# Up projection of groups two to four in seven block products, with the gate's sums of x and cached weight sums

## The chip, the cores and the metric

The kernel runs on one core of a Trainium2 chip. The metric is the device time of one execution in microseconds, the median of three runs. Inputs and outputs are float32; matmuls take float32r operands.

## The reference

The part that matters here is the first block's gated projection with a sparsity step: per row of s, the half of the entries that are smallest in magnitude is set to zero.

```python
s = silu(einsum('bsh,ih->bsi', x, w_gate))          # x: 2 x 1024 x 1024, w: 2752 x 1024
_, idx = top_k(-abs(s), k)                          # k = 1376 of 2752
s = s with the entries idx of each row set to 0
s = s * einsum('bsh,ih->bsi', x, w_up)
x = layernorm(x + einsum('bsi,hi->bsh', s, w_down))
# then a second block: low-rank-adapted feed-forward on x, and another layernorm
```

## The kernel before

**Tiling.** The 2048 rows are 16 tiles of 128, in four groups of four tiles. A group is worked on as two pairs of tiles. The 2752 columns are eight blocks of 344 (`BW`), taken as four block pairs `u` = 0 to 3. The contraction over 1024 is halved. So for a tile pair and a block pair, x and the weight are each 2x2 blocks: `A11` to `A22` of x, `B11` to `B22` of the weight.

**Products.** `products` multiplies one block of x (for both tile pairs) with one weight block. Every float32 operand is split into a rounded high part and a remainder (`split`: a cast on ScalarE, line 173, and a subtraction, line 174, mostly on GpSimd), and three of the four combinations are multiplied: 24 matmuls of 128x344 for one x block and one weight block over two tile pairs (line 353). Gate (other than group one's first block pair) uses seven block products for the eight of a plain 2x2 product: it multiplies blocks and sums of blocks of x (`S1` to `S4`) with blocks and sums of the weight (`T1` to `T4`), and `post` adds the products up from PSUM. Up uses the plain form: four steps of two block products each, 48 matmuls a step, and `up` multiplies the PSUM result with the gate's result.

**Steps.** `gate_up` (line 283) goes through a list of steps (group, block pair, gate or up, step). At each step it starts weight loads up to five steps ahead (`w_load`, into three raw slots `wr`), prepares weights up to three steps ahead (`w_prep`: cast and subtraction, into four slots each of `wh` and `wl`), emits the matmuls, and empties PSUM. PSUM has four pair buffers. A framework orders the instructions of each engine from this program order; what is emitted earlier has precedence where both are ready.

**Weight sums.** In group one, `w_prep` forms T1 to T4 of the gate's weights on VectorE and writes them to device memory: as one float32 tensor for the first block pair, as high and low parts for the other three. Later groups load them: the first block pair's are split again, the others go straight into `wh` and `wl` (line 258).

**Sums of x.** `x_raw` loads the next group's x into buffers that top-k has left, and `x_slot` forms one operand (sums on VectorE, cast on ScalarE, subtraction on VectorE). For the next group this happens in the last block pair, at the steps that the table `XAT` names.

**Top-k.** `topk` (line 417) is a generator. While group g is projected, it works on group g-1, one piece at each call: it loads the group's s, takes absolute values, makes six passes that count per row how many entries lie below a threshold (three tiles by a sign activation with accumulation on ScalarE, line 460, one on VectorE, line 463) and update the threshold, then selects by two VectorE operations per tile (lines 497 and 500), writes the mask (line 513), and checks the counts by a register read (lines 518 to 534). Its pieces are held behind the latest split and the latest PSUM reads by `behind`. `gate_up` calls it from the first step of a group's first block pair:

```python
for _ in range(2 if w == "u" and k % 2 == 0 else 1):
    if self.tkg:
        next(self.tkg, None)
```

All loads and stores are on SP's queue, in order. After `gate_up` come the down projection, its layernorm and the second block, which the change does not touch but for the steps at which the first three masks of the down projection are prepared.

Of the kernel before, what the change touches and what calls it, by code (L numbers as in the profile page):

```python
# [7 lines left out]
F = mybir.dt.float32  # L8
# [5 lines left out]
ALU = mybir.AluOpType  # L14
# [4 lines left out]
P = 128  # L19
# [18 lines left out]
T0 = 0.7528  # L38
SLOPE = 0.000528
TKAT = (0, "g", 0)  # L40
CACHED = ("T1", "T2", "T3", "T4")
# [5 lines left out]
WDG = 0  # L47
XAT = {"raw": (("g", 4), ("g", 5), ("g", 6), ("u", 0)), ("u", 0): ("S2",), ("u", 1): ("S1", "S3", "S4"), ("u", 2): ("A11", "A21"), ("u", 3): ("A12", "A22")}
WARM = 48
# [16 lines left out]
class Kern:  # L66
# [8 lines left out]
    def run(self):  # L75
# [3 lines left out]
        with ExitStack() as es:  # L79
# [14 lines left out]
            for i in range(8):  # L94
# [12 lines left out]
                (u, b): [self.dram.tile([P, CW], F, name=f"tw{u}{b}{n}") for n in "hl"] for u in range(NU) for b in CACHED  # L107
            }
            self.q1, self.q2, self.x2 = [], [], {}
            ps_es = ExitStack()  # L110
# [71 lines left out]
    def x_raw(self, g):  # L182
# [7 lines left out]
        for h in range(1 if g else 2):  # L190
# [8 lines left out]
            if g == 0 and h == 0:  # L199
                yield  # L200

    def x_slot(self, op):
        V, sub = self.nc.vector, ALU.subtract
# [14 lines left out]
    def form(self, i):  # L218
        g, u, w, k = self.steps[i]
        return 0 if w == "u" or g + u == 0 else 2 if g == 0 else 1  # L220

    def w_load(self, i):
# [12 lines left out]
        if f == 2:  # L235
            if k == 0:
                self.wb = {q: load(q) for q in G0}
            self.wraw.append(self.wb)
        elif f and u == 0 and b in CACHED:
            r = self.wr.get()  # L240
            self.lastd = nc.sync.dma_start(r, self.tw_d[u, b][0])
            self.wraw.append(r)
        elif f and b in CACHED:
            self.wraw.append(None)
        else:
            self.wraw.append(load(b))

    def w_prep(self, i):
# [21 lines left out]
        if g + u == 0 and w == "g" and k:  # L270
# [3 lines left out]
            for o, x, y in ((), T_AT[0], T_AT[1] + T_AT[2], T_AT[6])[k]:  # L274
                V.tensor_tensor(self.tt[o], self.b0[x], self.b0.get(y, self.tt.get(y)), ALU.subtract)
        if (g, u, w, k) == (0, 0, "u", 3):
            for o in CACHED:
                nc.sync.dma_start(self.tw_d[0, o][0], self.tt[o])
        if f == 2 and b in CACHED:
            for x, d in zip(hl, self.tw_d[u, b]):  # L280
                nc.sync.dma_start(d, x.bitcast(F))

    def gate_up(self):
        nc, V = self.nc, self.nc.vector
        ng = self.nt // GT
        self.steps = [(g, u, w, k) for g in range(ng) for u in range(NU) for w in "gu" for k in range(7 if w == "g" and g + u else 4)]
        self.xfull, self.tkg, self.xs, self.xraw, self.wraw, self.wq, self.li, self.wi = {}, None, {}, {}, [], [], 0, 0
# [4 lines left out]
        for i, (g, u, w, k) in enumerate(self.steps):  # L292
# [35 lines left out]
            if u == NU - 1 and g + 1 < ng:  # L328
                if (w, k) == XAT["raw"][0]:
                    self.xg = self.x_raw(g + 1)  # L330
                for _ in range(XAT["raw"].count((w, k))):
                    next(self.xg, None)
                for op in XAT.get((w, k), ()):
                    with self.behind():
                        self.x_slot(op)
# [21 lines left out]
    def post(self, un, k, x, cc):  # L357
# [734 lines left out]
```

## Time and profile before

| what | value |
|---|---|
| median of three runs | 1923.47 us (1922.35 to 1924.25) |
| profiled execution | 1926.91 us, span 1925.1 us |
| mean granted TensorE clock | 0.993 |
| TensorE busy | 1885.3 us, 10825 matmuls |
| line 353 (gate and up), three forms | 1928 matmuls each, 14.0 to 929.4 us from the span's start |
| VectorE, ScalarE, GpSimd busy | 1229.6, 904.0, 973.0 us |
| traffic | 488.66 MB, 254 GB/s over the span |

Times in the profile are microseconds from the start of one profiled execution. A group's row gives how often it ran, the busy time and the mean of one in ns, and after the bar the idle time of its engine just ahead of it with what ended it. A matmul's mean includes the time in which it overlaps its neighbours. A window's row gives the busy time of each engine in that stretch, the number of instructions in brackets, the granted clock, the share of the DMA engines' time and GB/s. A timeline's row gives start, duration, engine, line, operation, and in brackets the idle time ahead and what ended it.

### The profile page before, as it was taken

The page shows a single profiled execution, that of the slowest core. Times are in us where ns is not written, and L with a number is a line of the kernel's source. Part 1 is how long each engine was busy: PE and PEld are TensorE (multiplying, and loading weights), DVE is VectorE, ACT ScalarE, POOL GpSimd, SP SyncE. Part 2 cuts the span into 40 slices and gives each one's busy share as a digit, 9 for nine tenths or more (in the row PEclk, how much of TensorE's full clock was granted, in tenths as well). Part 3 has the DMA queues.
Part 4 walks back from the last instruction along what each step waited for, and adds up shares of the span by engine and source line. Part 5 has one row for each costly group of instructions (what it writes and reads, how often), then busy time and mean ns, then how long its engine had stood idle before and what let it go on. Part 6 is the DMA issues. An engine that isn't in the chain of part 4 may idle for free. (4 is left out here: it accounts for less than half of the span.)

```text
span 1925.1 us, 29381 instructions
## 1 busy us (share of the span) xinstructions
PE 1885.3 (98%) x10825; PEld 1754.4 (91%) x10825; DVE 1229.6 (64%) x1831; ACT 904.0 (47%) x1448; POOL 973.0 (51%) x606
## 2 busy tenths in 40 slices
PE   9999999999999999999999999999998999998998
PEld 9999999999999999999888787888787979898896
DVE  4633556767358574691238998688467857779565
ACT  4333477414883258622246533323333746557362
POOL 5655664445445354355565443554565746436062
PEclk9999999999999999999999999999999999999999
DMA  7677687676977868667798756977776878485651
GB/s 266 237 250 260 236 325 261 210 272 253 330 231 241 314 235 303 236 228 256 282 328 285 270 188 227 337 245 261 268 250 244 279 284 321 155 318 177 229 196 66
DMA packets 166205, 488.66 MB, mean 254 GB/s; under 512 B 24772, under 2 KB 45380, under 8 KB 166056
## 3 DMA queue, kind: packets, MB, share of 16 engines
q1 hardware_dynamic: 165848, 486.43, 71.9%
q8 instruction: 85, 1.39, 0.3%
q14 instruction: 64, 0.52, 0.1%
q10 hardware_dynamic: 208, 0.31, 0.0%
HBM read 370.30 MB, written 116.33 MB: 253 GB/s over the span
## 5 line engine op out<-in xcount | busy, mean ns | idle before, releaser
L174 POOL TENSOR_TENSOR wl<-wr,wh 128x1376 fp32r<-128x1376 f32 (+2 forms) x187 | 566.4, 3035 | 466.1 <-ACT wh L173 436.8
L353 PE MATMUL mm<-wh,xh 128*128 128x344 f32 x1928 | 610.4, 322 | 2.8 <-DMA wh<-tw3T1h 2.8
L353 PE MATMUL mm<-wh,xl 128*128 128x344 f32 x1928 | 609.8, 320 | 0.0
L173 ACT CAST wh<-wr 128x1376 fp32r<-128x1376 f32 (+2 forms) x192 | 232.4, 1215 | 340.9 <-PE mm L353 199.6
L353 PEld LDWEIGHTS mm<-wh,xh 128*128 128x128 f32 x1928 | 364.7, 189 | 3.0 <-issue 3.0
L353 PEld LDWEIGHTS mm<-wh,xl 128*128 128x128 f32 x1928 | 364.6, 189 | 0.0
L353 PE MATMUL mm<-wl,xh 128*128 128x344 f32 x1928 | 342.1, 319 | 0.0
L353 PEld LDWEIGHTS mm<-wl,xh 128*128 128x128 f32 x1928 | 310.1, 188 | 0.0
L765 PE MATMUL mm<-wh,mh 128*128 128x512 f32 x680 | 217.8, 400 | 0.1
L765 PE MATMUL mm<-wl,mh 128*128 128x512 f32 x680 | 215.1, 395 | 1.1 <-POOL wl L174 1.1
L765 PE MATMUL mm<-wh,ml 128*128 128x512 f32 x648 | 205.5, 396 | 0.8 <-DVE ml L750 0.8
L460 ACT ACTIVATE jk<-a,cur 128x2752 int8<-128x2752 f32 x66 | 170.8, 2588 | 31.2 <-DVE cur L482 15.8
L994 POOL TENSOR_TENSOR hf<-hf,gt 128x344 f32<-128x344 f32 x96 | 142.2, 1491 | 75.6 <-DVE gt L988 68.7
L725 POOL TENSOR_TENSOR m<-m,ub 128x512 f32<-128x512 f32 (+2 forms) x93 | 111.0, 1194 | 128.0 <-ACT ub L724 65.8
L981 PE MATMUL mm<-wh,fh 128*128 128x344 f32 x512 | 166.2, 325 | 5.8 <-DVE gt L988 5.2
L983 PE MATMUL mm<-wh,fl 128*128 128x344 f32 x512 | 164.0, 320 | 0.0
L982 PE MATMUL mm<-wl,fh 128*128 128x344 f32 x512 | 163.9, 320 | 0.0
L765 PEld LDWEIGHTS mm<-wl,mh 128*128 128x128 f32 x680 | 127.4, 188 | 30.1 <-POOL wl L174 2.2
L768 DVE TENSOR_TENSOR acc<-acc,mm 128x1024 f32<-128x1024 f32 x96 | 116.4, 1214 | 57.9 <-PE mm L765 27.8
L765 PEld LDWEIGHTS mm<-wh,mh 128*128 128x128 f32 x680 | 124.7, 189 | 24.8 <-ACT mh L749 0.5
L765 PEld LDWEIGHTS mm<-wh,ml 128*128 128x128 f32 x648 | 121.2, 189 | 26.9 <-DVE ml L750 1.0
L992 ACT ACTIVATE pa<-pa 128x344 f32<-128x344 f32 x256 | 123.0, 483 | 38.6 <-DVE pa L990 34.0
(191 smaller groups left out, 2742.5 us busy)
## 6 DMA issues: line engine op xcount, KB each, us to landing
wr<-wu SPq DMA_DIRECT2D x64, 688.0 KB
wr<-wg SPq DMA_DIRECT2D x52, 688.0 KB
wr<-wd SPq DMA_DIRECT2D x48, 512.0 KB
s_d<-cc SPq DMA_DIRECT2D x64, 344.0 KB
m_d<-mt SPq DMA_DIRECT2D x64, 344.0 KB
a<-s_d SPq DMA_DIRECT2D x64, 344.0 KB
wl<-wc_w SPq DMA_DIRECT2D x48, 344.0 KB
wh<-wc_w SPq DMA_DIRECT2D x48, 344.0 KB
```

The lines of the kernel that those rows point to most:

```text
L173: self.lasta = self.nc.scalar.copy(hi, raw)
L174: (eng or self.nc.gpsimd).tensor_tensor(lo, raw, hi.bitcast(F), ALU.subtract)
L353: self.nc.tensor.matmul(o, l, r, start=start and n < m and n % (2 * KH) == 0, stop=stop and n >= m and (n - m) % KH == KH - 1)
L460: nc.scalar.activation(jk.bitcast(I8), av[j], AF.Sign, bias=t, scale=-1.0, accum_out=s)
L725: nc.gpsimd.tensor_tensor(m[:, :w], m[:, :w], ub[:, :w], ALU.mult)
L765: nc.tensor.matmul(ps[:, h], a, b[:, h * 512 : (h + 1) * 512], start=i == 0, stop=i == len(ops) - 1)
L768: nc.vector.tensor_tensor(out, out, ps.rearrange("p a b -> p (a b)"), ALU.add)
L981: nc.tensor.matmul(o, fh[:, c, :], wh[:, c, :], start=c == 0, stop=False)
L982: nc.tensor.matmul(o, fh[:, c, :], wl[:, c, :], start=False, stop=False)
L983: nc.tensor.matmul(o, fl[:, c, :], wh[:, c, :], start=False, stop=False)
L992: nc.scalar.activation(pa[:, r], pa[:, r], AF.Copy, scale=0.5, accum_out=part[:, r, b : b + 1])
L994: G.tensor_tensor(hf[:, hs], hf[:, hs], gt, ALU.add)
```

## The change

In groups two to four, up takes the seven products of the gate's scheme: steps become 7 for 4, of 24 matmuls for 48, with the gate's operands of x. The new `upost` adds the products up in buffers of its own (a copy on ScalarE for the first product, seven additions from PSUM on VectorE) and then multiplies with the gate's result by four VectorE operations whose operands both lie in SBUF. The sums of up's weights are formed in group one by `w_prep`, at the third and fourth up step of each block pair, and written as float32; later groups load them and split them. The next group's x operands are formed at other steps, since up now uses all of them, and `A21` is formed no more for groups two to four. Top-k gets one call at each step. The first block pair's gate sums are written two steps earlier, and the first down masks are prepared at other steps.

```diff
+TKN = 1
-XAT = {"raw": (("g", 4), ("g", 5), ("g", 6), ("u", 0)), ("u", 0): ("S2",), ("u", 1): ("S1", "S3", "S4"), ("u", 2): ("A11", "A21"), ("u", 3): ("A12", "A22")}
+XAT = (
+    {"raw": (("g", 4), ("g", 5), ("g", 6), ("u", 0)), ("u", 0): ("S2",), ("u", 1): ("S1", "S3", "S4"), ("u", 2): ("A11",), ("u", 3): ("A12", "A22")},
+    {"raw": (("g", 4), ("g", 5), ("g", 6), ("u", 0)), ("u", 1): ("A11",), ("u", 2): ("S2",), ("u", 3): ("S1", "S3"), ("u", 4): ("A12",), ("u", 5): ("S4",), ("u", 6): ("A22",)},
+)
+            self.tu_d = {(u, b): self.dram.tile([P, CW], F, name=f"tu{u}{b}") for u in range(NU) for b in CACHED}
     def form(self, i):
         g, u, w, k = self.steps[i]
-        return 0 if w == "u" or g + u == 0 else 2 if g == 0 else 1
+        return 0 if g == 0 and (w == "u" or u == 0) else 2 if g == 0 else 3 if w == "u" else 1
...
-        elif f and u == 0 and b in CACHED:
+        elif b in CACHED and (f == 3 or u == 0):
             r = self.wr.get()
-            self.lastd = nc.sync.dma_start(r, self.tw_d[u, b][0])
+            self.lastd = nc.sync.dma_start(r, self.tu_d[u, b] if f == 3 else self.tw_d[u, b][0])
             self.wraw.append(r)
...
-        if (g, u, w, k) == (0, 0, "u", 3):
+        if (g, u, w, k) == (0, 0, "u", 1):
             for o in CACHED:
                 nc.sync.dma_start(self.tw_d[0, o][0], self.tt[o])
+        if g == 0 and w == "u":
+            self.b0[b] = raw
+            if k == 2:
+                tt = [self.tk.tile([P, 2, CW], F, tag=t, name="tu") for t in ("a0", "ku")]
+                self.tt = {f"T{j + 1}": tt[j // 2][:, j % 2] for j in range(4)}
+            for o, x, y in {2: T_AT[0], 3: T_AT[1] + T_AT[6] + T_AT[2]}.get(k, ()):
+                V.tensor_tensor(self.tt[o], self.b0[x], self.b0.get(y, self.tt.get(y)), ALU.subtract)
+                nc.sync.dma_start(self.tu_d[u, o], self.tt[o])
...
-        self.steps = [(g, u, w, k) for g in range(ng) for u in range(NU) for w in "gu" for k in range(7 if w == "g" and g + u else 4)]
+        self.steps = [(g, u, w, k) for g in range(ng) for u in range(NU) for w in "gu" for k in range(7 if g or (w == "g" and u) else 4)]
...
-                self.post((g, u), k, ps, cc)
+                (self.upost if w == "u" else self.post)((g, u), k, ps, cc)
...
-            for _ in range(2 if w == "u" and k % 2 == 0 else 1):
+            for _ in range(TKN):
                 if self.tkg:
                     next(self.tkg, None)
-            if (g, u, w) == (ng - 1, NU - 1, "u") and k > 1:
+            if (g, u, w) == (ng - 1, NU - 1, "u") and k in (3, 5):
                 next(self.d0)
...
+    def upost(self, un, k, x, cc):
+        nc, V = self.nc, self.nc.vector
+        if k == 0:
+            self.mt = [self.ev.tile([P, NPR, 2, BW], F, tag=f"cc{t}", bufs=2, name=f"mt{t}") for t in range(2)]
+        c, s = self.mt, cc[un]
+        c11, c12, c21, c22 = (c[i // 2][:, :, i % 2] for i in range(4))
+
+        def add(o, a):
+            self.lastv = V.tensor_tensor(o, x, a, ALU.add)
+
+        def mult(i):
+            o, b = c[i // 2][:, :, i % 2], s[i // 2][:, :, i % 2]
+            self.lastv = V.tensor_tensor(o, o, b, ALU.mult)
+
+        if k == 0:
+            nc.scalar.copy(c11, x)
+        elif k == 1:
+            add(c12, c11)
+        elif k == 2:
+            add(c21, c12)
+        elif k == 3:
+            add(c12, c12)
+            add(c22, c21)
+        elif k == 4:
+            add(c11, c11)
+            mult(3)
+        elif k == 5:
+            add(c12, c12)
+            mult(0)
+            mult(1)
+            self.put(self.mp_d, un, 0, c[0])
+        else:
+            add(c21, c21)
+            mult(2)
+            self.put(self.mp_d, un, 1, c[1])
```

More of the change, by code (lines that the diff above doesn't have):

```diff
@@ L200, in x_raw, with x_ops @@
                 yield
+    def x_ops(self, ops):
+        for op in ops:
+            with self.behind():
+                self.x_slot(op)
     def x_slot(self, op):
@@ L328, in gate_up @@
             if u == NU - 1 and g + 1 < ng:
-                if (w, k) == XAT["raw"][0]:
+                xat = XAT[g > 0]
+                if (w, k) == xat["raw"][0]:
                     self.xg = self.x_raw(g + 1)
-                for _ in range(XAT["raw"].count((w, k))):
+                for _ in range(xat["raw"].count((w, k))):
                     next(self.xg, None)
-                for op in XAT.get((w, k), ()):
-                    with self.behind():
-                        self.x_slot(op)
+                self.x_ops(xat.get((w, k), ()))
+            if g > 1 and (u, w) == (0, "g"):
+                self.x_ops(XAT[1].get(("n", k), ()))
             if g and (u, w, k) == TKAT:
                 self.tkg = self.topk(g - 1)
-            for _ in range(2 if w == "u" and k % 2 == 0 else 1):
+            for _ in range(TKN):
                 if self.tkg:
                     next(self.tkg, None)
-            if (g, u, w) == (ng - 1, NU - 1, "u") and k > 1:
+            if (g, u, w) == (ng - 1, NU - 1, "u") and k in (3, 5):
                 next(self.d0)
```

## The prediction

> **What bounds the kernel now.** I read the page first, then the costliest groups, the table of windows over the second group's eight stages (four block pairs, gate and up in turn), and last the timelines of ScalarE, VectorE and GpSimd in those stages.
>
> The page and its groups say that TensorE has hardly any idle time, and that in gate and up (line 353) it waited once, 2.8 us:
>
> ```profile
> PE 1885.3 (98%) x10825; PEld 1754.4 (91%) x10825; DVE 1229.6 (64%) x1831; ACT 904.0 (47%) x1448; POOL 973.0 (51%) x606
> L353 PE MATMUL mm<-wh,xh 128*128 128x344 f32 x1928 | 610.4, 322 | 2.8 <-DMA wh<-tw3T1h 2.8
> ```
>
> So a matmul taken away is time won, as long as the others keep up. The time of one is not the mean of 322 ns (matmuls overlap) but the distance between starts. Two successive products of 24 matmuls:
>
> ```profile
> 273.62 1.42 PE L353 MATMUL mm<-wl,xh 128*128 128x344 f32 x8
> 277.39 1.42 PE L353 MATMUL mm<-wl,xh 128*128 128x344 f32 x8
> ```
>
> give 3.77 us; over a group it is 3.78 us, or 157.5 ns a matmul. I call 3.78 us a step's time from here on. The windows of the second group (gate and up of the first and second block pair, gate of the third) show who has room beside TensorE:
>
> ```profile
> core 0: us, PE busy (x) PEld busy (x) DVE busy (x) ACT busy (x) POOL busy (x), PEclk, DMA share, GB/s
> 244.80:271.30 26.50, 26.50 (x170) 26.50 (x170) 13.81 (x12) 15.27 (x14) 18.76 (x6) 1.00 0.97 354
> 271.30:301.50 30.20, 30.20 (x194) 30.20 (x193) 12.59 (x36) 27.14 (x22) 10.07 (x4) 1.00 0.91 319
> 301.50:328.00 26.50, 26.50 (x170) 26.50 (x170) 14.37 (x29) 21.85 (x19) 15.88 (x5) 1.00 0.73 238
> 358.20:384.70 26.50, 26.50 (x170) 26.50 (x170) 25.75 (x14) 8.63 (x7) 16.84 (x5) 1.00 0.65 213
> 384.70:414.90 30.20, 30.20 (x194) 30.20 (x193) 26.57 (x27) 4.02 (x4) 10.80 (x3) 1.00 0.71 232
> ```
>
> Not everyone has. ScalarE is 90% busy in the first up stage, where top-k counts signs, and VectorE 97% and 88% in the third pair's stages, where top-k looks for its threshold. The clock is full; nothing is to be had there. The timeline gives top-k's ends in this group: first sign count, last sign count, and the first work after its register check.
>
> ```profile
> 275.67 2.59 ACT L460 ACTIVATE jk<-a,cur 128x2752 int8<-128x2752 f32 x1
> 350.33 2.59 ACT L460 ACTIVATE jk<-a,cur 128x2752 int8<-128x2752 f32 x1
> 359.02 3.08 DVE L497 SCALAR_TENSOR_TENSOR ku<-a,hi 128x2752 f32<-128x2752 f32 x1
> 415.39 1.66 DVE L403 TENSOR_TENSOR mt<-mm,cc 128x688 f32<-128x688 f32 x2 [3.81 <-DVEq L530]
> ```
>
> This is a serial chain of 415.39-275.67 = 139.7 us. In the third group it is 138.8 us (503.1 to 641.9).
>
> **Matmuls.** In three groups, for four block pairs each, up falls from 8 block products to 7: 3x4x24 = 288 matmuls by 157.5 ns = 45.4 us, 15.1 us a group. This is sure, because line 353 has no idle time to be eaten first.
>
> **The top-k chain.** Its pieces are tied to steps in program order. The first sign count is call 8, the register check call 38. Before, the up steps were 7.56 us long and every second one took two calls; calls 8 to 38 lay over two gate and three up stages. Now each step takes one call, and calls 8 to 38 have steps 8 to 38 of 3.78 us. Queued behind a late top-k piece on VectorE are the adds that empty PSUM (four buffers: a step can start when the product four steps back is read), behind a late sign count on ScalarE the casts of the weights. TensorE waits for both. Room: the 8th step begins at 271.3; 32 steps end at 271.3+121.0 = 392.3, when the product behind the check can be read; it must be read 3 steps later, at 403.6. From the first count, 403.6-275.7 = 127.9 us.
>
> What the chain needs: 139.7, less what it now waits for TensorE's pace. That is 5.4 us ahead of 359.02 (the last count's result was ready at 353.6), and 1.7 and 1.3 us of ScalarE idle between counts where a cast waited for its slot: 131.3 us stay. Added:
> - ScalarE, to the last count: 5 more weight casts (13 for 8, since up has three more products a pair) at 1.24 us from start to start, and two more PSUM copies at 0.62: 7.4 us. Some fit in the 1.3 to 2.5 us that ScalarE waits for each update of the thresholds; I take 6, ends 3.7 and 7.4.
> - VectorE, from there to the check: 11 PSUM adds for 9 reads, at 0.79: 1.6; three products with the gate (two SBUF operands) at 0.87: 2.6; one more add ahead of the buffer's release: 0.8. Sum 5.
> - Waits of these products on GpSimd: below.
>
> These three lines show that price: a VectorE operation on two SBUF tensors, of 0.16 us elsewhere, ended with GpSimd's subtraction, while an add that reads PSUM ran beside one undisturbed.
>
> ```profile
> 329.52 3.16 POOL L174 TENSOR_TENSOR wl<-wr,wh 128x1376 fp32r<-128x1376 f32 x1 [1.89 <-ACT wh L173]
> 329.67 3.04 DVE L488 TENSOR_TENSOR num<-num,df 128x4 f32<-128x4 f32 x1
> 317.44 0.86 DVE L372 TENSOR_TENSOR cc<-mm,cc 128x688 f32<-128x688 f32 x1
> ```
>
> The nearest row in shape, line 990 (128x688, two SBUF operands), has a median of 0.876 and a longest of 2.97 us. So a product waits between 0 and 3.2 us (one subtraction); three of them 0 to 9.5; I take 3.5, since GpSimd is idle about half of that time. The Trainium skill, "SBUF — State Buffer", section "Who interferes with whom", says that a VectorE instruction with two SBUF inputs and a GpSimd instruction reading SBUF hold one port in turn, for the whole instruction, and that PSUM operands stay out of it. It speaks against putting these products beside the subtractions: were each to meet one, the sum would be 3x(9.5-3.5) = 18 us higher; by line 990's median, 3x3.5 = 10.5 us lower.
>
> Chain: 131.3+6+5+3.5 = 145.8 us. It overruns the room by 17.9 us a group, which TensorE waits: 53.7 us for three. Ends: 10.5 (2.9 us of the second idle go, for 1.3; 3.7 added on ScalarE, 5 on VectorE, no waits: 138.4 us) and 25.3 (7.4, 5 and 9.5 added: 153.2 us).
>
> **Weights' splits and the port between groups.** Up now splits 7 blocks on GpSimd for 4. At 3.16 us against 3.78 they fit. In the last up stage of groups two and three, the sums of x for the next group come beside them: 14 subtractions and 8 sums at 0.64 us, with four products at 0.87, are 17.6 us, and 7x3.16 = 22.1 of GpSimd, 39.7 on one port in 26.5 us: 13.2 over. A split may be 10.4 us late before TensorE waits for it (from its slot's release to the third step's last eight matmuls, less cast and split). 2.8 us are left, twice: 5.6, ends 0 and 11. One operand of x is no longer formed: part of the same count.
>
> **Group one.** Four VectorE subtractions (1.6 to 4.6 us each, by lines 267 and 275) and four 688 KB writes a pair, beside up steps of 7.56 us. SP's loads behind them wait, because B11 and B21 hold two of three raw slots until the sums are formed. Following the loads of the first pair, the next gate's blocks land about 10 us later than now (58 for 48 us), and its second product starts at 78. I take nothing: that cover is about 10 us; without it each pair costs what exceeds it. Moving the first pair's write ahead and changing which up steps prepare the down stage are also nothing by the same cover.
>
> **DMA.** Up loads 3 more blocks a pair, 24.8 MB for 12 pairs. The only crowded place is a group's first pair (0.97 and 0.91 above): rival two.
>
> **Sum.** The profiled execution took 1926.91 us (span 1925.1 and 1.8 around it). 1926.9-45.4+53.7+5.6 = 1940.8; the median of the runs is 3.4 us lower, so 1937.
>
> **Rivals.** *One, faster: the chain fits.* If ScalarE's casts fall wholly into its waits and VectorE's products seldom meet GpSimd, the chain is shorter. The place is the register check, and the point that decides is 143.0 us (127.9+15.1): below it each group gains. With 129.7+0+5 = 134.7 us the overrun is 6.8 and the time 1923.5-45.4+20.4 = 1898; with no overrun 1878. For it: ScalarE idles 13 us between counts now. Against it: those idles follow VectorE's updates, and more of those meet GpSimd now. *Two: loads decide in each first pair.* 26.5x354+30.2x319 is 19.0 MB in 56.7 us; three more blocks make 21.1 MB in 52.9 us, 399 GB/s, where 354 at a share of 0.97 makes 365 the most. That costs 57.8-52.9 = 4.9 us a group; behind the same chain it adds up to 14.7: 1952. Against it: one up load was already issued early, and the second pair has room (0.73). *Three: group one's cover is gone*, and three pairs wait some 5 us each for their gate's weights, also 1952. That the matmuls would not fall is excluded by the step list.
>
> **How the numbers follow.** A measurement of this kernel tells about 0.2% (3.8 us) from no change. Forecast 0.53, of which 0.10 lies within 0.2% (an overrun of 12 to 14.5 us) and 0.43 above; rival one 0.27; rival two 0.12; rival three 0.08. Faster 0.27, same 0.10, slower 0.63. Range: 1898 (rival one's price, no port cost between groups) to 1965 (overrun 25.3 is 75.9, port 11: 1923.5-45.4+86.9); beyond it some 0.1 on either side.
>
> **What would show it.** Line 353 with 96 fewer of each of three forms, its last start near 943 for 929.4; TensorE waiting some 15 us a group, most of it on VectorE's adds between the second pair's up and the third pair's up; the chain from first count to check near 146 us; GpSimd over 80% busy in up. Wrong if TensorE's idle time at that line stays below 30 us, if it waits mostly for DMA, or if the waits lie in group one.

## The result and the profile after

The changed kernel took 2010.3 us (median of 4 runs, 2002.3 to 2016.9), the kernel before 1922.9 beside it: 4.55% slower, ratio 1.0455 with a 95% interval of 1.0424 to 1.0485, or 87 us. The forecast was slower, but by 14 us, and its range ended at 1965. The profiled execution took 2016.9 us (span 2014.8) for 1926.9.

The page of the changed kernel: busy times, the granted clock in 40 slices, and the group of gate and up (line 372 now, which was 353).

```profile
PE 1880.7 (93%) x10537; PEld 1734.8 (86%) x10537; DVE 1397.1 (69%) x1925; ACT 952.9 (47%) x1490; POOL 1113.2 (55%) x642
...
PEclk9999999989999999999989999999999999999999
...
L372 PE MATMUL mm<-wh,xh 128*128 128x344 f32 x1832 | 596.9, 330 | 87.5 <-DVE mt L411 42.0
```

The 288 matmuls are gone (96 of each form), yet TensorE is busy for almost as long as before (1885.3 us). It waited 87.5 us at this line where it had waited 2.8, and the mean of a matmul rose from 322 to 330 ns: waits and slow matmuls, not work. Half of the waiting was for line 411, the adds of `upost` that empty PSUM.

A measure that all kernels below share is the **loss**: the time from the first to the last product of gate and up in the trace, less 3.78 us for each of them. Before: 241 products, from 13.98 to 925.76, 911.8 - 240x3.78 = 4.6 us. After: 229 products, 14.63 to 1004.54, 989.9 - 228x3.78 = 128.1 us. Of that, 91.5 are TensorE's waits at the line's forms, and the other 36.6 are slow steps: matmuls whose starts lie more than 0.2 us apart, without a wait between, sum to 36.8 us beyond the usual distance. So gate and up became 128.1 - 4.6 - 12x3.78 = 78 us longer; some 11 us came behind them (the span goes on for 1008.0 us after the last start of that line, where it went on for 997.1).

The windows of group two in the changed kernel, around the end of top-k's chain:

```profile
core 0: us, PE busy (x) PEld busy (x) DVE busy (x) ACT busy (x) POOL busy (x), PEclk, DMA share, GB/s
383.00:410.00 27.00, 22.36 (x140) 21.85 (x139) 25.02 (x24) 13.15 (x12) 17.47 (x5) 0.99 0.80 311
410.00:436.00 26.00, 26.00 (x158) 26.00 (x158) 25.93 (x16) 9.85 (x8) 19.77 (x6) 0.95 0.60 202
436.00:463.00 27.00, 17.46 (x98) 16.92 (x97) 18.07 (x25) 3.32 (x3) 6.29 (x2) 0.81 0.52 206
```

VectorE is full in the first two windows (25.02 us of 27, 25.93 of 26), as in the third pair before, and in the third the queue behind it has emptied TensorE: 17.46 busy us of 27, and the clock falls to 0.81 there. The longest wait of each group (8.28, 8.23, 8.25 us) is for an add that stands behind four of top-k's mask operations (line 568) in a row, from 432.24 us on here; in the kernel before, two PSUM reads ran in the middle of the four. The last of the four, the adds, and the matmul that waited:

```profile
441.24 3.08 DVE L568 TENSOR_SCALAR_CACHE_REDUCE ku<-a,thr 128x2752 uint8<-128x2752 f32 x1
444.24 2.43 DVE L411 TENSOR_TENSOR mt<-mm,mt 128x688 f32<-128x688 f32 x3
446.04 0.63 PE L372 MATMUL mm<-wh,xh 128*128 128x344 f32 x1 [8.28 <-DVE mt L411]
```

The chain's three ends in that group, first sign count, last sign count, first work after the register check:

```profile
295.94 2.59 ACT L515 ACTIVATE jk<-a,cur 128x2752 int8<-128x2752 f32 x1
386.39 2.59 ACT L515 ACTIVATE jk<-a,cur 128x2752 int8<-128x2752 f32 x1
459.90 0.88 DVE L411 TENSOR_TENSOR mt<-mm,mt 128x688 f32<-128x688 f32 x1 [8.79 <-DVEq L585]
```

The chain takes 164.0 us (161.5 and 164.1 in the next groups), not 139.7 and not the predicted 145.8. I call first to last sign count the sign phase (90.4, 93.9, 94.8 us; before 74.7, 74.0, 73.8) and the rest VectorE's phase (73.5, 67.6, 69.3; before 65.1, 64.8, 67.0).

### The profile page after: what moved, and what is told of

It reads as the page before. It is cut to its first block, busy times and chain, and to the rows that moved or that the text cites. A ratio compares the mean times of both kernels' runs of the same rounds, so it can differ in the third digit from the quotient of the medians.

```text
span 2014.8 us, 29207 instructions
## 1 busy us (share of the span) xinstructions
PE 1880.7 (93%) x10537; PEld 1734.8 (86%) x10537; DVE 1397.1 (69%) x1925; ACT 952.9 (47%) x1490; POOL 1113.2 (55%) x642
## 5 line engine op out<-in xcount | busy, mean ns | idle before, releaser
L179 POOL TENSOR_TENSOR wl<-wr,wh 128x1376 fp32r<-128x1376 f32 (+2 forms) x223 | 705.5, 3177 | 440.5 <-ACT wh L178 349.4
L372 PE MATMUL mm<-wh,xh 128*128 128x344 f32 x1832 | 596.9, 330 | 87.5 <-DVE mt L411 42.0
L372 PE MATMUL mm<-wh,xl 128*128 128x344 f32 x1832 | 593.1, 327 | 0.0
L372 PEld LDWEIGHTS mm<-wh,xh 128*128 128x128 f32 x1832 | 357.5, 195 | 96.6 <-issue 33.4
L178 ACT CAST wh<-wr 128x1376 fp32r<-128x1376 f32 (+2 forms) x228 | 280.3, 1235 | 316.7 <-PE mm L372 195.8
L372 PEld LDWEIGHTS mm<-wh,xl 128*128 128x128 f32 x1832 | 357.6, 195 | 0.0
L372 PE MATMUL mm<-wl,xh 128*128 128x344 f32 x1832 | 328.7, 322 | 4.0 <-DMA wl<-tw3T1l 2.7
L372 PEld LDWEIGHTS mm<-wl,xh 128*128 128x128 f32 x1832 | 298.9, 190 | 5.2 <-DMA wl<-tw3T1l 3.0
L1049 POOL TENSOR_TENSOR hf<-hf,gt 128x344 f32<-128x344 f32 x96 | 142.3, 1493 | 71.7 <-DVE gt L1043 64.8
L1036 PE MATMUL mm<-wh,fh 128*128 128x344 f32 x512 | 166.1, 325 | 5.4 <-DVE gt L1043 5.2
L820 PEld LDWEIGHTS mm<-wl,mh 128*128 128x128 f32 x680 | 128.1, 189 | 31.4 <-POOL wl L179 3.2
```

The costliest lines, as they stand in the source:

```text
L178: self.lasta = self.nc.scalar.copy(hi, raw)
L179: (eng or self.nc.gpsimd).tensor_tensor(lo, raw, hi.bitcast(F), ALU.subtract)
L372: self.nc.tensor.matmul(o, l, r, start=start and n < m and n % (2 * KH) == 0, stop=stop and n >= m and (n - m) % KH == KH - 1)
L820: nc.tensor.matmul(ps[:, h], a, b[:, h * 512 : (h + 1) * 512], start=i == 0, stop=i == len(ops) - 1)
L1036: nc.tensor.matmul(o, fh[:, c, :], wh[:, c, :], start=c == 0, stop=False)
L1049: G.tensor_tensor(hf[:, hs], hf[:, hs], gt, ALU.add)
```

## The experiments

Kernels of one batch ran with the kernel before on the same chip; times are medians, ratios are against that kernel.

### What the change costs without top-k, and what without x

```diff
 # both kernels: top-k keeps its loads, Abs, mask count and stores; its calls stay in number
-        for p in range(NPASS): ... counts, updates, selections, register check
+        for _ in range(NPASS * 3 + 7):
+            yield
```

**The changed kernel so cut.**

> The changed kernel with top-k's six passes, selection and check left out (loads, absolute values, one mask operation a tile and the mask writes stay, at the same calls; the mask is that of a first guess). Theory (top-k's chain and the PSUM reads wait for each other on VectorE, and this makes most of the loss): TensorE then loses only what the trace shows outside the chain: about 13 us in group one, 11 us at each of two group boundaries, 6 to 10 us at the start of down, against 45.4 us of matmuls won. That is within 8 us of the kernel before without top-k (b_notopk), some 85 us below the changed kernel. Rival (loads, casts and subtractions of seven weight blocks are what is too slow): it stays 40 us or more above b_notopk.

**The kernel before so cut.**

> The kernel before with the same parts of top-k left out. Both theories: TensorE waited 2.8 us in gate and up before, so the time stays within 8 us of the kernel before (1923); it is the reference for a_notopk.

Measured: 1915.5 us (ratio 0.9956, 0.9939 to 0.9973) and 1916.9 (0.9973, 0.9961 to 0.9985). Top-k costs the kernel before 6 us and the changed kernel 95. But without it the change still wins 1.4 us instead of 45: some 44 us go elsewhere. The cut kernel's loss is 43.2 (3.2 in the kernel before so cut): 11.4 in group one and 2.0 where group two begins, 11.9 and 11.6 where groups three and four begin, and 6 in all the rest. Two waits at the first of these boundaries:

```profile
478.13 0.63 PE L372 MATMUL mm<-wh,xh 128*128 128x344 f32 x1 [4.42 <-DVE mt L411]
490.62 0.40 PE L372 MATMUL mm<-wh,xh 128*128 128x344 f32 x1 [1.98 <-DVE mt L411]
```

In the next run groups three and four also use group two's x again:

```diff
-            if u == NU - 1 and g + 1 < ng:
+            if u == NU - 1 and g == 0:
                 xat = XAT[g > 0]
```

> The changed kernel without top-k's passes, selection and check, and with groups three and four using group two's operands of x again (their x isn't loaded, summed or split; both parts are left out). If the sums of x beside the splits cost what the two boundaries showed without top-k (waits of 4.4 and 2.0 us, of 4.1 and 3.3 us, and slow steps behind them), the time falls from 1915 by 18 to 25 us, to 1890 to 1897, and what is left above the 1871 that 45.4 us of matmuls would leave is group one's 16 us and a few us at the start of down. If the boundaries cost only the 5.6 us of the prediction, it stays at 1907 or above.

Measured: 1892.5 us (0.9836, 0.9812 to 0.9861), 23 us less, inside the first forecast. Both boundaries are free now (0.1 us of loss each). So the work on x (its loads, sums and splits, which this run leaves out together) costs 11.5 us a boundary, and the wait is for line 411: PSUM adds that stand behind the work on x on VectorE. GpSimd has a share in it. Ahead of the wait of 4.42 us, two subtractions for x took 3.38 and 3.62 us, for 0.68 elsewhere, while GpSimd split two weights; the second one, the splits, and the late add:

```profile
471.59 3.62 DVE L179 TENSOR_TENSOR xl<-xt,xh 128x512 fp32r<-128x512 f32 x1
467.93 6.73 POOL L179 TENSOR_TENSOR wl<-wr,wh 128x1376 fp32r<-128x1376 f32 x2 [4.25 <-ACT wh L178]
477.12 0.86 DVE L411 TENSOR_TENSOR mt<-mm,mt 128x688 f32<-128x688 f32 x1
```

### Group one's weight sums alone

```diff
 # the kernel before, with tu_d, the earlier write of the first pair's sums, and in w_prep:
+        if g == 0 and w == "u":
+            self.b0[b] = raw
+            for o, x, y in {2: T_AT[0], 3: T_AT[1] + T_AT[6] + T_AT[2]}.get(k, ()):
+                V.tensor_tensor(self.tt[o], self.b0[x], self.b0.get(y, self.tt.get(y)), ALU.subtract)
+                nc.sync.dma_start(self.tu_d[u, o], self.tt[o])
```

> The kernel before with only the change's work in group one: up's weight sums formed and written there, nothing else changed, and nobody reads them. The prediction's step: 0, the cover holds. What the trace of the changed kernel suggests: about 13 us more (two waits of 5.7 and 3.0 us on VectorE's PSUM reads, with slower matmuls after each), so 1936.

Measured: 1939.2 us (1.0096, 1.0067 to 1.0126), 15.8 us slower; the loss is 21.1 for 4.6. The prediction had taken nothing, since its cover of 10 us was one for loads. The wait is another: TensorE stands behind an up product on VectorE. In the changed kernel, VectorE's queue and the step that waits for it:

```profile
67.24 1.58 DVE L277 TENSOR_TENSOR tw<-wr 128x1376 f32<-128x1376 f32 x1
68.74 0.87 DVE L458 TENSOR_TENSOR mt<-mm,cc 128x688 f32<-128x688 f32 x1
```
```profile
69.66 0.65 PE L372 MATMUL mm<-wh,xh 128*128 128x344 f32 x1 [5.66 <-DVE mt L458]
```

The up product (line 458) releases PSUM, but the gate's weight sums for the next pair (line 277) stand ahead of it. These are late themselves: they start at 62.43 us for 48.73 in the kernel before, since the first of their loads is issued at 52.38 for 40.48, behind stores of up's sums.

### What a wait costs TensorE

In the kernel before, an extra 128x128 matmul at four up steps of group one waits for a row of small VectorE operations:

```diff
+                r = {(1, 0): 0, (1, 2): 8, (2, 0): 16, (2, 2): 30}.get((u, k)) if g == 0 and w == "u" else None
+                if r is not None:
...
+                    V.tensor_copy(z, (cc[g, u][1][:, 0, 1] if k == 0 else self.mt[1][:, 0, 0])[:, :P])
+                    for _ in range(r):
+                        V.tensor_scalar(z, z, 1.0, None, ALU.mult, ALU.add, accum_out=za)
+                    nc.tensor.matmul(ps[0][:, 0, :P], z, self.ident, start=True, stop=True)
```

> The kernel before, with four waits put into TensorE's work in group one: at up steps of the second and third block pair one extra 128x128 matmul waits for a row of 1, 9, 17 and 31 small VectorE operations that starts behind the latest PSUM read, so that TensorE stands for about 1, 2, 3 and 6 us (the extra product falls on values that the next product overwrites). Theory one, a wait costs more than itself, because the granted clock falls behind it: the short waits are followed by steps of the usual length (7.56 us), the two long ones by 1.5 to 3 us more in the next steps; the sum is 12 us of waits and 3 to 6 us of slow clock, 1936 to 1942. Theory two, a wait costs itself alone: 1933 to 1936, no step behind a wait longer than before.

Measured: 1975.4 us (1.0272, 1.0250 to 1.0294). The waits came out longer than meant, 3.55, 7.22, 14.52 and 14.54 us, 39.8 in all, so the forecast times don't apply, but the question is answered. The steps with the waits and the ones behind them lost 49.5 us against 3.79 us a step. Less the waits and 0.42 us for each extra product, 8.0 us are left: 2.0 us for each wait. Taken from the matmuls whose starts lie more than 0.2 us apart, they are 1.3, 2.7, 2.0 and 1.3 us in the order of the waits. The windows around the second one:

```profile
122.00:129.80 7.80, 0.59 (x4) 0.32 (x3) 6.94 (x19) 0.75 (x1) 4.13 (x1) 0.74 0.44 181
129.80:135.00 5.20, 5.19 (x19) 5.20 (x20) 0.00 (x0) 0.00 (x0) 0.00 (x0) 0.50 0.00 0
135.00:139.20 4.20, 4.20 (x25) 4.20 (x25) 0.00 (x0) 0.00 (x0) 0.00 (x0) 0.88 0.00 0
139.20:143.00 3.80, 3.80 (x26) 3.80 (x25) 0.00 (x0) 1.35 (x1) 2.10 (x1) 1.00 0.37 151
```

For 5.2 us behind the wait nothing else runs and TensorE is never idle, yet the granted clock is 0.50 and matmuls start every 0.29 us instead of 0.158. The price doesn't grow with the wait. The changed kernel's own waits fit: 1.5 us more behind 2.65 us at 409.6, 1.6 behind 3.01 at 105.5, 2.5 behind 5.66 at 69.7, and 2.0, 2.9 and 2.2 behind the three of over 8 us; none behind 1.74 (977.2) or 2.49 (629.2). In the traces of all runs here, no wait of 0.8 to 1.8 us in gate and up was followed by more than 0.7 us of slow steps, some of those between 1.8 and 3.6 us were, and every one above 3.6 us was, by 1.2 to 2.9 us.

### Which part of the chain grew

Two lines of ScalarE's groups, restricted to group three's sign phase, first before, then after:

```profile
L460 ACT ACTIVATE jk<-a,cur 128x2752 int8<-128x2752 f32 x18 | 46.6, 2586 | 8.1 <-DVE cur L490 5.0 <-DVE cur L482 2.9
L173 ACT CAST wh<-wr 128x1376 fp32r<-128x1376 f32 x9 | 12.0, 1337 | 4.2 <-PE mm L353 2.9 <-issue 1.3
```
```profile
L515 ACT ACTIVATE jk<-a,cur 128x2752 int8<-128x2752 f32 x18 | 46.6, 2588 | 20.3 <-DVE cur L545 13.4 <-DVE cur L537 6.8
L178 ACT CAST wh<-wr 128x1376 fp32r<-128x1376 f32 x17 | 22.6, 1335 | 0.2
```

The counts themselves take the same 46.6 us. Of the 19.9 us that the phase grew, 10.6 are casts (17 for 9) and 12.2 are longer waits for the next threshold; the casts' own waits gave 4.0 back, and 1.1 is other work. VectorE's small threshold updates show one reason for the waits: 5, 5 and 7 of the 71 in a sign phase took over 0.7 us, 15.2, 12.1 and 16.6 us together, where before it was one in each group, 3.0 us. The next runs took these apart.

**Products without a second SBUF operand.** The four products with the gate become operations on one SBUF operand (the product is left out):

```diff
...
-            self.lastv = V.tensor_tensor(o, o, b, ALU.mult)
+            self.lastv = V.tensor_scalar(o, o, 1.0, None, ALU.mult, ALU.add, accum_out=ac)
```

> The changed kernel with the four multiplications by the gate's result replaced by multiplications by 1.0 with one SBUF operand and an accumulator, of the same size (the product with the gate is left out). Prediction's step: the three products in the chain wait 3.5 us a group on GpSimd, so 10 us less. Theory that the port decides: each product waits about 2 us, and the sign counts' updates behind them too: 25 us or more less. Theory that VectorE's order alone decides: under 10 us less.

Measured: 1991.2 us (1.0359, 1.0332 to 1.0386), 19 less, between the forecasts. But the sign phase stayed at 84.8, 96.1 and 93.0 us: the products ran undisturbed (0.85 to 0.87 us), and the threshold update behind them met GpSimd in their place. VectorE's two last update instructions, of 0.16 us elsewhere, and GpSimd beside them:

```profile
558.88 3.16 DVE L537 TENSOR_TENSOR cur<-cur,lo 128x4 f32<-128x4 f32 x1
562.08 3.06 DVE L538 TENSOR_TENSOR cur<-cur,hi 128x4 f32<-128x4 f32 x1
```
```profile
558.86 6.26 POOL L179 TENSOR_TENSOR wl<-wr,wh 128x1376 fp32r<-128x1376 f32 x2 [0.64 <-ACT wh L178]
```

It is no chance meeting. When the last sign count ends, ScalarE turns to the casts queued behind it, these start GpSimd's subtractions, and just then VectorE computes the update that ScalarE waits for.

**Weight sums loaded in two parts.** The sums of up's weights go from memory straight into the split slots: in one run both slots (no cast, no subtraction), in the other only the low slot (no subtraction, the cast stays). Both move the same bytes in groups two to four.

```diff
 # both slots: tu_d holds two tensors, form 3 takes the path of line 254
-        elif b in CACHED and (f == 3 or u == 0):
+        elif b in CACHED and f == 1 and u == 0:
...
 # the low slot only
+        if f == 3 and b in CACHED:
+            self.lasta = nc.scalar.copy(hl[0], raw)
+            nc.sync.dma_start(hl[1].bitcast(F), self.tu_d[u, b])
...
```

> The changed kernel, with up's four weight sums stored as two tensors and loaded in groups two to four straight into the two split slots, so that 4 casts on ScalarE and 4 subtractions on GpSimd a block pair are gone and 4 loads of 688 KB come in their place (both tensors hold the float32 sum, so the low part's values are left out). Theory one, the casts between the sign counts and the port that GpSimd holds are what lengthens the top-k chain: with 7 casts in place of 13 in its window the chain falls from 161 to 164 us to about 140, the sign phase from 91 to 95 us to about 75, and the time falls from 2010 by 50 to 80 us, to 1930 to 1960, in spite of the loads. Theory two, the seven steps themselves (more PSUM reads and the products with the gate on VectorE, one top-k piece a step): the chain stays above 155 us and the time above 1985. Rival, loads: a first pair then moves 23.9 MB in 52.9 us, 452 GB/s where 365 was the most seen; that would cost up to 12.7 us a group (38 us), shown by waits of TensorE on loads in the first pair of groups two to four.

> The changed kernel with 4 GpSimd subtractions a block pair replaced by loads straight into the low slot, while the 4 casts on ScalarE stay (the loaded low part is the float32 sum itself, so the low part's values are left out). It moves the same bytes in groups two to four as the kernel whose casts are gone too (1984), and differs from it in those casts alone. Theory one, the casts lengthen the sign phase: it stays at 88 to 95 us here where that kernel had 75 to 77, and the time is 1990 to 2010. Theory two, GpSimd's hold of the port makes the sign phase long, by late threshold updates: the sign phase falls below 82 us and the time to 1985 or below.

Measured: 1983.7 us (1.0314, 1.0289 to 1.0339) without casts, 2001.7 (1.0425, 1.0394 to 1.0456) with them. Without casts the sign phase is back at 76.4, 76.8 and 75.4 us, as theory one said, but the time is not: from 275 to 301 us, in group two's first pair, 379 GB/s moved with the DMA engines 99% busy, TensorE now waited for weights too (8.4 us for `tw3`, 4.0 for `tu0`), and group one, which now writes up's sums twice, lost 15.8 us (13.1 in the changed kernel) and the start of group two 10.9 (2.1). Mechanism and rival both held. With casts the phase was 77.1, 86.7 and 88.7 us, with 16 casts and 16.5 us of threshold waits in group three: taking only the subtractions away gives a part.

**Subtractions in halves.** Every weight split's subtraction on GpSimd becomes two of 128x688:

```diff
...
+            self.lasta = nc.scalar.copy(hl[0], raw)
+            for q in range(2):
+                z = slice(q * CW // 2, (q + 1) * CW // 2)
+                nc.gpsimd.tensor_tensor(hl[1][:, z], raw[:, z], hl[0][:, z].bitcast(F), ALU.subtract)
```

> The changed kernel with GpSimd's subtraction of every weight split in gate and up cut into two of 128x688. Theory one, the threshold updates are late because VectorE's instructions wait for whole subtractions of GpSimd (single updates of 128x4 took 3.1 us for 0.16, one right after the other): halves release the port after 1.6 us, so ScalarE's waits for updates in a sign phase fall from 20 us to 12 to 15, the sign phase from 90-95 to 83-89 us, and the time by 15 to 35 us, to 1975 to 1995. Theory two, the updates are late because they queue behind PSUM reads and products: nothing moves, 2002 to 2018.

**The same in the kernel before.**

> The same cut in the kernel before, as a control. Both theories: TensorE waits for none of these there, so 1919 to 1926; the longest of the small VectorE updates falls from 2.4-3.2 us to about 1.6 if the port goes over at the end of an instruction.

Measured: 1983.6 us (1.0312, 1.0290 to 1.0335), 27 less, and in the kernel before 1923.9 (1.0008, 0.9998 to 1.0018): nothing. In groups three and four the sign phase fell to 87.6 and 85.8 us and the threshold waits to 15.9 and 15.2, in group two neither fell (91.8; 21.2). The longest late update in the sign phases fell to 1.67 us (1.59 in the kernel before), as expected: the port goes over at the end of an instruction. But while GpSimd has more halves to do, the next update waits for the next half. In group three four updates in a row took 1.65, 1.64, 1.60 and 1.60 us (0.16 elsewhere) beside four halves, and 13 updates were late, 19.2 us together, where whole subtractions had made 5 late, 12.1 us. The last of the four, and the halves:

```profile
558.91 1.60 DVE L543 TENSOR_TENSOR cur<-cur,hi 128x4 f32<-128x4 f32 x1
553.38 7.12 POOL L285 TENSOR_TENSOR wl<-wr,wh 128x688 fp32r<-128x688 f32 x4 [0.42 <-ACT wh L282]
```

The clearest gain was in group one, whose loss fell from 13.1 to 2.7; the wait of 5.66 us above became this one:

```profile
65.76 0.43 PE L378 MATMUL mm<-wh,xh 128*128 128x344 f32 x1 [1.45 <-DVE mt L464]
```

So the length of one hold on the port decides how late a single VectorE operation is, but not how late a row of small updates is. Of the 27 us, 10 are group one's; why the threshold waits fell in two groups of three isn't shown.

### More room for the chain

One more step between the sign counts and the update, in the first three or in all six passes:

```diff
+            if p < 6 and g < self.nt // GT - 1:     # p < 3 in the other run
+                yield
```

> The changed kernel with one more step between the pieces of top-k in each of the first three passes: the register check comes at call 41 in place of 38 in groups two to four, so the room grows by 3 steps, 11.3 us a group. Theory, the chain overruns its room and TensorE waits for the excess: the waits shrink by that much in each group, and some of the slow steps behind them go too: 34 to 45 us less than 2010, 1965 to 1976. Rival, the VectorE work around the chain is itself too much wherever the chain lies: less than 15 us gained.

> The same with one more step in each of the six passes: the check at call 44, the room 22.7 us a group larger. A pass then has four steps, 15.1 us, which is what a pass took in the changed kernel (90.5 to 94.8 us for six), so that no sign count should queue late. Theory, overrun: 68 to 85 us less than 2010, 1925 to 1942, and what is left over 1900 to 1915 is VectorE's phase. Rival, the end of the chain then meets the sums of x of the last block pair (x is loaded from step 46) and the boundaries grow: 1950 or above, with the waits at the group's end.

> Both together: one more step in each of the six passes and the halved subtractions. Theory one: 1987 less 10 to 25, 1962 to 1977, most of it at the x sums between groups, whose 24 us of VectorE work meet the same subtractions. Theory two: 1980 to 1990.

Measured: 2000.1 us (1.0414, 1.0393 to 1.0435), 1987.3 (1.0343, 1.0324 to 1.0363), and with halves 1975.3 (1.0275, 1.0258 to 1.0292). The first two fell short of the overrun theory's times and lie where their rivals put them; the third lies inside its first forecast, but its gain was not at the sums of x. Chain, room and loss show why (us; chain of groups two, three, four; the room is 127.9 plus 3.78 for each added step; "boundaries" is the loss around the starts of groups three and four, and the last column what is left without these, group one and group two's start; where a part ends is set to a few us):

| kernel | chain | chain less room, summed | loss | boundaries | loss in the groups |
|---|---|---|---|---|---|
| changed | 164.0, 161.5, 164.1 | 106 | 128.1 | 21.5 | 91 |
| halves | 158.6, 152.5, 154.3 | 82 | 104.5 | 17 | 83 |
| 3 steps more | 166.9, 163.6, 161.1 | 74 | 115.5 | 22 | 82 |
| 6 steps more | 166.5, 166.2, 165.8 | 47 | 102.8 | 33 | 58 |
| 6 steps and halves | 167.1, 166.1, 165.0 | 46 | 95.5 | 40 | 51 |

The groups' loss follows chain less room over all five: 60 us less of the one goes with 40 us less of the other. But each added step only partly shortens a queue: a count that may not come before its step makes the chain longer where it wasn't late. And the chain's end moves into the last pair, where the sums of x are: the boundaries grew from 21.5 to 33 and 40 us, the rival's case.

### Seven products in some of the ups

**In the last pair of group four alone, then in the last pair of groups two to four** (the kernel before, with the predicate below for form 3 in up; the others keep the plain form and two calls at every second step):

```diff
+    def seven(self, g, u):
+        return g == 3 and u == NU - 1      # g > 0 and u == NU - 1 in the second
```

> The kernel before, with seven products in one up only, the last block pair's of group four: no top-k piece, no x for a next group and no later gate lie beside it; group one forms the weight sums for this one pair. Theory: 24 matmuls less are 3.8 us, and where nothing serial lies beside the ups the scheme's win shows: 1919 to 1921 (one pair's forming in group one may cost up to 4 us of it, since 15.8 us were measured for four pairs). Rival, the seven steps cannot be fed even there (sums from memory, PSUM reads, products with the gate): same or slower, 1923 or above.

> The kernel before with seven products in the up of the last block pair of groups two to four alone: behind top-k's check, beside the next group's x in groups two and three. 72 matmuls less are 11.3 us. Against it stand the two boundaries, 22 us by the comparison of the two kernels without top-k and without x (1915 to 1892), and group one's forming for one pair, which left 10 us of loss in the kernel with the last up alone. Theory, prices add: 1923 - 11.3 + 22 + 10 + 3.8 (that kernel's own gain, already in its 10) = 1940 to 1950. Rival, the boundaries were dear only because the other ups lie beside them: 1915 to 1930.

Measured: 1932.9 us (1.0052, 1.0025 to 1.0080) and 1953.9 (1.0180, 1.0146 to 1.0214), some 4 us above what adding the prices gave. The first was expected to win 3.8 and lost 10. Its profiled execution is the fastest of its runs (1927.0), and there the loss is 8.8 for 4.6, so the saved step was given back, 2.6 us around the start of group two and 1.6 at the wait for a load near the end; where the slower runs lost more, no trace shows. The second has its loss (40.4 us) at the boundaries, 12.9 and 16.9, around the start of group two, 3.0, and at the end, 5.4 (a load; 4.6 before); its groups lose next to nothing. These ups lie behind top-k's check, so the boundaries are dear by themselves.

**In the first three pairs of groups two to four, with halves and six added steps**, the version that the prices point to; in the second run three of the six steps lie between the selections:

```diff
+        return g > 0 and u < NU - 1
```

> A version put together from the prices: seven products in the ups of the first three block pairs of groups two to four only, the last block pair plain, with its x sums at the steps of the kernel before and two calls of top-k at every second up step there; one more step in each of top-k's six passes; GpSimd's split subtractions halved. 216 matmuls less are 34.0 us. Against it: group one's forming 3 to 5 us with the halves, the chain 5 to 8 us a group as in the changed kernel with both measures. If the boundaries are free again as in the kernel before: 1923 - 34 + 20 to 29 = 1909 to 1918. If the end of the chain, now in the last pair's gate, meets the x sums: 10 us a boundary more, 1929 to 1938.

> The same, with three of the six added steps between the selections instead of after the sign counts: VectorE's phase took 71 to 73 us in 13 steps of 3.78 (49 us) in the changed kernel with both measures, the sign phase 92 to 95 in 24. If VectorE's phase is the one that overruns: 3 to 8 us below the version with all six in the passes. If the sign phase is, 5 to 15 us above it.

Measured: 1940.4 us (1.0085, 1.0061 to 1.0109) and 1946.7 (1.0128, 1.0102 to 1.0153). Of 87 us lost, 18 are left with 216 of the 288 matmuls still saved, just above the dearer of the two forecasts. It beats the changed kernel but not the one before. TensorE still waits at each place named: 2.98 us in group one, 4.01 and 2.93 at the boundaries, 3.4 to 3.7 us at a threshold update in each group. With the steps between the selections it was 6 us slower, as the sign phase's overrun would have it.

## Why the prediction was wrong in size

**Matmuls: right.** 96 fewer of each form, 45.4 us.

**The chain: the mechanism was right, one term was mis-sized.** The formula (chain less room is what TensorE loses) holds roughly: 164.0 - 127.9 = 36.1 us, 33.6 and 36.2 in the next groups, 106 in all, where the two kernels with and without top-k differ by 95; and with more room the loss fell by two thirds of what the formula gives (the table above). The prediction put 17.9 a group, because its chain was 145.8 us. VectorE's phase was nearly as predicted: 65.1 - 5.4 + 5 + 3.5 = 68.2, measured 67.6 to 73.5 (VectorE stood idle 8.8, 6.0 and 7.6 us at the register check, for 3.8, 3.6 and 5.8 before; why wasn't looked into). The failed step is "6, ends 3.7 and 7.4" on ScalarE. The sign phase was put at 74.7 - 3.0 + 6 = 77.7 us and was 90.4 to 94.8, so that this term, put at 6, was some 19 to 23. Three things were missed:
- Five casts more were counted; eight were there in group three, because a longer phase holds more steps, and their casts lengthen it again.
- The casts were to fall into ScalarE's waits for the thresholds. But those waits grew, from 8.1 to 20.3 us, since the update on VectorE stood behind added PSUM reads and products.
- Port waits were priced only for three products behind the last count. The small updates are on the port as well (12.1 to 16.6 us of late ones a group), and come just when the casts have started GpSimd.

VectorE's timeline ahead of the threshold for which ScalarE waited 6.78 us in group three shows the last two together, an update (line 525) behind three adds and two products (line 415), where 0.88 and 0.16 us would be the undisturbed times:

```profile
566.78 1.65 DVE L411 TENSOR_TENSOR mt<-mm,mt 128x688 f32<-128x688 f32 x2
568.35 0.14 DVE L519 TENSOR_SCALAR cur<-cur 128x1 f32<-128x1 f32 x1
568.47 1.46 DVE L415 TENSOR_TENSOR mt<-mt,cc 128x688 f32<-128x688 f32 x1
569.85 0.86 DVE L411 TENSOR_TENSOR mt<-mm,mt 128x688 f32<-128x688 f32 x1
570.75 2.98 DVE L415 TENSOR_TENSOR mt<-mt,cc 128x688 f32<-128x688 f32 x1
573.65 3.13 DVE L525 TENSOR_SCALAR up<-cur 128x4 int32<-128x4 f32 x1
```

The rule that the prediction quoted from the Trainium skill, "SBUF — State Buffer", section "Who interferes with whom", was the right one to weigh. The sum by it, 18 us higher, erred on the same side as the prediction, because it too was applied to the products alone.

**The slow clock: a missing term.** 36.6 of the 128.1 us are slow steps, nearly all right behind a wait, not waits. The trace of before showed it: its one wait of 2.8 us was followed by 1.5 us of slow matmuls. The Trainium skill, "TensorE: Matmul & The Clock Gate", section "What's actually happening", says that the clock halves after an idle window of about 3.4 us and comes back after a busy one. The halved clock (0.50 in the window above) and its stay of 3 to 6 us agree; the idle time doesn't quite, since here some waits from 1.8 us on already cost it and others up to 3.6 us did not, and the measurement decides. Where a wait is a queue's, as in group one, they come on top of it (2.5 behind 5.66 us); whether the overrun of the chain already contains them isn't shown.

**Between the groups: wrong.** 5.6 us were put for two boundaries, 11 at most; 23 were measured. The sum of port time (39.7 us in 26.5) asked when a split would be late. But TensorE waited for PSUM adds that stood on VectorE behind the work on x, two of whose subtractions were held up by GpSimd (3.38 and 3.62 us for 0.68). The port was short, as summed, but what it made late was the adds: without top-k, TensorE waited 13.8 us for them at the two boundaries and 1.6 for GpSimd's splits in all of gate and up. The 10.4 us of slack belonged to the splits.

**Group one: wrong.** 0 was put, 15.8 measured. Rival three had a like price (some 5 us for each of three pairs), for weights that land late. They were late (the first load issued at 52.38 us for 40.48), but what TensorE waited for was an up product that stood behind their sums on VectorE, a queue that GpSimd's holds lengthened: with halves group one lost 2.7 us for 13.1.

**DMA: right.** TensorE waited 4.4 us for loads. Rival two's place, the first pairs, was busy, but only the run that loaded still more was held up there.

**The sum again**, in medians: 1922.9 - 45.4 + 15.8 + 23.0 + (94.8 - 6.0) = 2005, and 2010 were measured. Some 5 us stay. The profiled execution, the slowest of the four, has 11 us more behind gate and up, with TensorE's clock at 0.90 in the first 50 us of down, 0.93 before; no run looked into them. Of the signs that were to show the prediction right, the 96 matmuls, the waits on VectorE's adds and the lateness at the check came; the last start was 1006.8 for 943, the chain took 161.5 to 164.1 us for 146, waits lay in group one and between groups too, and GpSimd was 76% busy at most in the windows shown.

## What to carry to other kernels

When a step on the busiest engine gets shorter, what lies beside it gets denser: price a serial chain across engines with the queue ahead of each of its links and the casts that the longer chain itself will collect, not with the added work alone. Ask of every operation that empties PSUM what stands ahead of it on its engine; the longest waits in group one, between the groups and at the end of top-k's chain were each for a PSUM read behind something else on VectorE. And add to each wait of TensorE above some 2 us the slow steps that can follow it, 1.2 to 2.9 us by the traces here.

## What was not expected of the hardware

- Behind a wait the granted clock was half for 3 to 6 us whatever the wait's length: 1.3, 2.7, 2.0 and 1.3 us of loss behind 3.55, 7.22, 14.52 and 14.54 us.
- A VectorE update on 128x4 took 3.13 us for 0.16 beside GpSimd's subtraction even where it had one SBUF operand and a constant (the last row above), and two updates with two SBUF operands in a row took 3.16 and 3.06 us.
- Cutting GpSimd's subtractions in two cost the kernel before nothing (1923.9 for 1922.7) and took 27 us off the changed kernel, although the late updates in its sign phases took longer together (19.2 us for 12.1 in group three).
